# Two graph layers on one Trainium2 core: the first loads reordered, two of the first right sums made by ScalarE and accumulating transfers, and P5 placed between the turnings of the last adjacency chunks

## The chip, the cores and the metric

The kernel runs on one core of a Trainium2 chip. The metric is the time of the whole program on the device in microseconds. Five engines work side by side, each with a queue of its own: TensorE (PE in the profile; PEld is its loading of weights), VectorE (DVE), ScalarE (ACT), GpSimd (POOL) and SyncE (SP). [...]SP, ACT and POOL also issue transfers (DMA), which are carried out apart from the engines.

## The reference

The inputs are x, of shape (16, 1024, 128) in float32, a (1024, 1024) matrix `adj`, and small weights. Both layers are a graph step with a residual and a layer normalization:

```python
def gnn0(x):                       # first layer
    support = einsum('bnf,fo->bno', x, weight)
    return einsum('nm,bmo->bno', adj, support) + bias

def step(h):                       # second layer, 5 times
    m = einsum('nm,bmd->bnd', adj, h)          # both halves of av are this
    av = concatenate([m, m], axis=-1)
    u3 = h @ u3_w.T + u3_b
    z = sigmoid(av @ w3_w.T + w3_b + u3)
    r = sigmoid(av @ w4_w.T + w4_b + u3)
    hv = tanh(av @ w5_w.T + w5_b + (r * h @ u5_w.T + u5_b))
    return (1 - z) * h + z * hv

x = layernorm(x + gnn0(x))
x = layernorm(x + five_steps(x))
```

So each of the 16 batches is multiplied by `adj` six times. The change lies in the very first of these products.

## The kernel before

**Tiling.** The 16 batches go in four groups ("quads") of four. For a quad the product with `adj` is done by a Strassen-like scheme of two levels. At the outer level the matrix is taken as blocks and sums of blocks, `outer[1]` to `outer[7]`: 1 and 2 are the upper blocks, 4 and 7 the lower ones as they come out of the turning, and 3, 5 and 6 are the sums `s4`, `s1`, `s2`. Each outer product is done by an inner level of seven products, P1 to P7, with left sides `left[n][1..7]` and right sides `right[1..7]`. Outer products 1 and 2 are done together by one `chain`; then 3; then 6 and 7; then 5 and 4. PSUM banks `pa`, `pb`, `pc` hold the inner products.

**The right sides.** In the first chain, with `rows` holding x0 to x3 (the four batches of the quad), P1 and P2 read x0 as it is, P3 reads x1 as it is. P5, P6, P7 and P4 read the four right sums, in `inner[0]`, made by `inner_sums` (lines 326 to 331): the first is x1 less x0 (the first block of each, for both halves of the rows), the second is x1's other block less the first sum, the third is x1's other block less x1's first block, the fourth is x0's other block less the second sum. Each is a DVE instruction of 128x512.

**The left sides.** `adj` comes in eight chunks of 512 KB and must be transposed on chip. `turn_adj(c)` does it for one chunk: for each of its two halves, four transposes on PE into a PSUM bank, and one copy from the bank into `blk`, by DVE or by ACT. The banks come from `bank()`, a rotation over three. P1 and P2 need chunks 0 and 1 only. `first_rest` turns chunks 2 and 3, and then `inner_left_12` makes the left sums of outer products 1 and 2 on DVE, four instructions of 128x1024 (lines 188 to 191; the second is the left side of P5, the third that of P6). `turn_rest` turns chunks 4 to 7. `outer_s1` makes `s1` in two halves (line 756; the first reads chunks 4 and 5, the second 6 and 7), line 751 makes `s2`, `outer_s4` makes `s4` in two halves (line 795).

**Sums by transfer.** `added_sums`, `added_left` and `added_t4` make a difference without DVE: ACT writes the negative of one operand, and a transfer issued by POOL adds the other operand to it from memory (`accum_op=ALU.add`). They serve the outer right sums in `tsum` and the left sums in `outer[7]`.

**Order.** [...]`tc.keep_in_program_order(op)` pins `op` behind the instruction that was traced just before it on the same engine; `tc.issue_after` pins a group behind a given one. In the first chain the order of the inner products is (1, 2, 5, 6, 7, 3, 4), and `hooks[12][a]` lists what is called ahead of product `a`. All DVE work named above is pinned, and so are the transposes of chunks 0 to 3; the inner products of the first chain and the transposes of chunks 4 to 7 are not. The copies of line 207 on ACT are not pinned either.

**Loads.** Line 127 issues the first loads: the first six alternate between the queues of SP and ACT, the rest go by SP. In the order of that line, SP issues chunk 0, x0, chunk 2, then chunks 4 to 7, x2, x3; ACT issues chunk 1, x1, chunk 3.

Of the kernel before, what the change touches and what calls it, by code (L numbers as in the profile page):

```python
# [12 lines left out]
ALU = mybir.AluOpType  # L13
# [7 lines left out]
def kernel(  # L21
# [32 lines left out]
    nc = tc.nc  # L54
    B, N, D = x.shape
    P = 128
    C = N // P
# [3 lines left out]
    CH = C // 2  # L61
# [10 lines left out]
    rows = const.tile([P, QUAD, N], F32, name="rows")  # L72
# [5 lines left out]
    inner = [const.tile([P, 4, 2, QT], F32, name=f"inner{i}") for i in range(2)]  # L78
# [16 lines left out]
    def bank(name, i=None):  # L95
        if i is None:
            i = turns[0]
            turns[0] = (i + 1) % 3
        return ps_m.tile([P, HALF], F32, tag=f"g{i}", name=name)
# [15 lines left out]
    def x_rows(b):  # L115
        return x[b].rearrange("(p c) d -> p (c d)", c=C)
# [7 lines left out]
    adj_rows = adj.rearrange("(h p n c) m -> n h p c m", h=2, n=4, c=2)  # L124
    raws = [agg[:, c] if c < CH else hid[:, c - CH] for c in range(C)]

    for i, c in enumerate([0, 1, "x0", "x1", *range(2, C), "x2", "x3"]):
        queue = queues[i % 2 if i < 6 else 0]
        if isinstance(c, str):
            k = int(c[1])  # L130
            queue.dma_start(rows[:, k], x_rows(k))
        else:
            queue.dma_start(raws[c], adj_rows[c // 2, c % 2])
# [10 lines left out]
    s1 = const.tile([P, CH, HALF], F32, name="s1")  # L144
    s2 = const.tile([P, CH, HALF], F32, name="s2")
    s4 = const.tile([P, CH, HALF], F32, name="s4")
    outer = {
        1: blk[0][:, 0], 2: blk[0][:, 1], 3: s4, 4: blk[1][:, 1], 5: s1, 6: s2, 7: blk[1][:, 0],
    }
# [34 lines left out]
    def inner_left_12():  # L184
        a = [[blk[0][:, :, 2 * j : 2 * j + 2, ts(i, QT)] for j in range(2)] for i in range(2)]
        put = tc.keep_in_program_order
        (a11, a12), (a21, a22) = a
        put(nc.vector.tensor_sub(e12[:, :, 3], a11, a21))
        put(nc.vector.tensor_add(e12[:, :, 0], a21, a22))
        put(nc.vector.tensor_sub(e12[:, :, 1], e12[:, :, 0], a11))  # L190
        put(nc.vector.tensor_sub(e12[:, :, 2], a12, e12[:, :, 1]))

    def turn_adj(c):
        cols = raws[c].rearrange("p (q k) -> p k q", k=C)
        i, at = divmod(c, CH)
        for j in range(2):
            pt = bank(f"pt_adj_{c}_{j}")
            pt3 = pt.rearrange("p (k q) -> p k q", k=CH)
            for k in range(CH):
                op = nc.tensor.transpose(pt3[:, k, :], cols[:, j * CH + k, :], ident)  # L200
                if c < CH:
                    tc.keep_in_program_order(op)
            dst = blk[i][:, j, :, ts(at, P)]
            if j == 0 and i == 0:
                tc.keep_in_program_order(nc.vector.tensor_copy(dst, pt3))
            else:
                nc.scalar.copy(dst, pt3)
# [118 lines left out]
    def inner_sums(xs, dst):  # L326

        yield nc.vector.tensor_sub(dst[0], xs(0, 1), xs(0, 0))
        yield nc.vector.tensor_sub(dst[1], xs(1, 1), dst[0])
        yield nc.vector.tensor_sub(dst[2], xs(1, 1), xs(0, 1))  # L330
        yield nc.vector.tensor_sub(dst[3], xs(1, 0), dst[1])

    def blocks_of(src, ns):

        if ns in ((1, 2), (3,)):
            v = src.rearrange("p b (h j x) -> p b h j x", h=2, j=2)
            if ns == (1, 2):
                return lambda j, k: v[:, k, :, j]
            return lambda j, k: v[:, 2 + k, 1:2, j]
        at = {(6, 7): slice(1, 3), (5, 4): slice(0, 4, 3)}[ns]  # L340
        return lambda j, k: tsum[:, at, k, ts(j, QT)]

    def sums_of(src, ns, pinned=False):
        t = inner[0 if ns in ((1, 2), (6, 7)) else 1]
        for op in inner_sums(blocks_of(src, ns), [t[:, i, : len(ns)] for i in range(4)]):
            if pinned:
                tc.keep_in_program_order(op)
        return op

    def first_sums(src):  # L350
        return inner_sums(blocks_of(src, (1, 2)), [inner[0][:, i] for i in range(4)])
# [339 lines left out]
    def call(f, *args):  # L691
        return lambda: f(*args)
# [20 lines left out]
    def added_sums():  # L713


        v = [
            x[2 * i : 2 * i + 2].rearrange("b (p c) d -> p b (c d)", c=C)[:, :, ts(j, HALF)]
            for j in range(2) for i in range(2)
        ]
        (lo, hi), ((lo0, hi0), (lo1, hi1)) = (rows[:, 0:2], rows[:, 2:4]), (v[:2], v[2:])  # L720
        put = tc.keep_in_program_order
        def added(i, negative, rest):
            put(nc.scalar.mul(tsum[:, i], negative, -1.0))
            put(nc.gpsimd.dma_start(tsum[:, i], rest, accum_op=ALU.add))

        added(2, hi[:, :, :HALF], hi1)
        yield
        added_left()
        added(0, lo[:, :, :HALF], hi0)
        yield  # L730
# [12 lines left out]

    rooms = [rows, hid]

    def turn_rest():
        for c in range(CH, C):
            turn_adj(c)
            if c % 2:
                outer_s1(c // 2 - 2)  # L750
        tc.keep_in_program_order(nc.vector.tensor_sub(s2, s1, outer[1]))

    def outer_s1(at):
        cols = ts(at, QT)
        tc.keep_in_program_order(
            nc.vector.tensor_add(s1[:, :, cols], outer[7][:, :, cols], outer[4][:, :, cols])
        )

    def first_rest():
        for c in range(2, CH):  # L760
            turn_adj(c)
        inner_left_12()

    def steps_of_sums(ns):
# [3 lines left out]
    def take(steps, n):  # L768
        for _ in range(n):
            op = tc.keep_in_program_order(next(steps))  # L770
        return op
# [4 lines left out]
    by_transfer = added_sums()  # L776
# [21 lines left out]
    for q in range(NQ):  # L798
        room = rooms[q % 2]
        hooks = {}  # L800
        if q == 0:
            hooks[12] = {
                2: [first_rest],
                5: [turn_rest, call(next, by_transfer)],
                7: [call(outer_s4, 0), call(take, sums3, 1), call(next, by_transfer)],
                3: [call(outer_s4, 1)],
                4: [
                    call(take, steps, 1)
                    for steps in (left3, left3, sums3, sums3, left3, left3, sums3)
                ] + [sum_t2],  # L810
            }
            hooks[3] = {7: [added_t4]}
            hooks[67] = {1: [rest_67]}
            layer0_weights()
            sums_of(rows, (1, 2), True)
        else:
            hooks[12] = projections(q - 1)
            hooks[12][6] += [
                call(sums_of, room, (3,), q == 1),
                call(outer_sums, room, False, True, q == 1),  # L820
            ]
            if q == 1:
                hooks[12][1].append(call(outer_sums, room, "lo", False, True))

        def fetch(q=q):
            drain(99, 0)
            if q == 0:

                for dst, b in [(hid[:, k], QUAD + k) for k in range(QUAD)] + [
                    (ypad[k], k) for k in range(2)  # L830
                ]:
                    tc.keep_in_program_order(nc.gpsimd.dma_start(dst, x_rows(b)))
                load_layer1_weights()
                return
            for k in range(2):
                nc.sync.dma_start(ypad[k], x_rows(q * QUAD + k))
            if q + 1 < NQ:
                load(q + 1, rooms[(q + 1) % 2], x_rows)
            else:
                load(0, rows, saved_rows)  # L840

        def ahead(room):
            with tc.issue_after(last_start[0].ins):
                sums_of(room, (1, 2))
                outer_sums(room, True, False)

        hooks.setdefault(67, {})["end"] = [fetch]
        hooks[54] = {7: [call(ahead, rooms[(q + 1) % 2])]}
        if q == 0:
            steps = first_sums(rooms[1])  # L850
            hooks[54] = {
                7: [call(take, steps, 2)],
                (3, (0,)): [
                    call(take, steps, 2), call(outer_sums, rooms[1], "hi", False, True),
                ],
            }
        if q != 1:
            then = f"12_x{q + 1}" if q + 1 < NQ else "12_0_0"
            hooks[54][4] = [call(head, then, rooms[(q + 1) % 2])]
        if q == 1:  # L860
            hooks[54][5] = [layer1_weights]
            hooks[54][4] = [turn_weights]
        if q == 0:
            aggregate(f"x{q}", room, hooks, False, (1, 2, 5, 6, 7, 3, 4), start_67)
        else:
            aggregate(f"x{q}", room, hooks, False)
# [199 lines left out]
```

## Time and profile before

| what | value |
|---|---|
| time, median of 3 runs | 1766.96 us (1766.76 to 1766.97) |
| the profiled execution: its own time | 1767.13 us |
| its span in the profile | 1764.9 us |
| PE busy | 1753.4 us, 6709 matmuls |
| DVE busy | 1302.2 us, 2286 instructions |
| ACT busy | 800.8 us, 1425 instructions |
| POOL busy | 110.4 us, 153 instructions |
| from start to P1's first matmul | 8.61 us |
| PE's last hole in the first 60 us | 0.60 us, ending at 11.17 us |
| mean granted clock of PE | 0.998 |

The span is what the profiler saw from the first to the last instruction; the program's time has 2.2 us more around it. Rows of a timeline give start, duration, engine, line, operation, output and input, the number of instructions merged into the row, and in brackets the idle time ahead of it and what ended it. Rows of the waits view give who waited for whom, the microseconds in total, the times, and the longest.

### The profile page before, as it was taken

To read this page: it belongs to the slowest core of one execution; us is meant where nothing else is said; L and a number is where in the kernel's file an instruction comes from. 1 tells how busy PE (TensorE), PEld (TensorE's weight loads), DVE (VectorE), ACT (ScalarE), POOL (GpSimd) and SP (SyncE) were. 2 spreads that over 40 slices of the span, in tenths; PEclk is the share of its full clock that TensorE was granted. 3 is DMA by queue.
4 is the path that set the end of the run, shared out by engine and by line. 5 is a ranking of instruction groups with operands and counts; after the bars stand their busy time and mean duration, and the time that the engine had idled before them with its cause. 6 is when DMAs were issued, how large, how long until landed. Compare 5 with 4: busy or idle time off the path is not lost.

```text
span 1764.9 us, 19957 instructions
## 1 busy us (share of the span) xinstructions
PE 1753.4 (99%) x6709; PEld 1264.9 (72%) x6709; DVE 1302.2 (74%) x2286; ACT 800.8 (45%) x1425; POOL 110.4 (6%) x153
## 2 busy tenths in 40 slices
PE   9999999999999999999999999999999999999998
PEld 8888885776858577685867758576675857668584
DVE  7977777676776857777778667777778577777778
ACT  4355554344353433435354452535445353443537
POOL 2312320000000000000000000000000000000004
PEclk9999999999999999999999999999999999999999
DMA  9244354051332505143351424324243240514232
GB/s 266 75 139 144 120 142 109 12 119 34 86 69 67 140 18 136 39 118 75 81 132 60 108 60 96 87 69 119 58 110 101 55 94 26 131 25 107 60 84 95
DMA packets 405604, 161.86 MB, mean 92 GB/s; under 512 B 388352, under 2 KB 389504, under 8 KB 405504
## 3 DMA queue, kind: packets, MB, share of 16 engines
q1 hardware_dynamic: 402960, 153.01, 34.2%
q0 software_dynamic: 1968, 5.77, 1.3%
q10 hardware_dynamic: 576, 1.84, 0.3%
q8 instruction: 53, 0.87, 0.2%
q14 instruction: 47, 0.39, 0.1%
HBM read 94.51 MB, written 65.01 MB: 90 GB/s over the span
## 4 chain that ended last, share of the span: by engine, by line
PE 99%; DMA 1%; DVE 0%; POOL 0%; issue 0%; SPq 0%; POOLq 0%; ACT 0%; DVEq 0%
PE pb L425 25%; PE pc L425 14%; PE pa L425 14%; PE pu L553 8%; PE ph L576 8%; PE ph L577 8%; PE pu L535 8%; PE seeded L568 8%; PE pc_x L425 3%; PE pa_x L425 3%; PE seeded L509 2%; DMA agg<-in_adj_dram 1%; PE pt_adj L200 0%; PE pt L667 0%; PE pt_end L941 0%
## 5 line engine op out<-in xcount | busy, mean ns | idle before, releaser
L425 PE MATMUL pb<-e,inner 128*128 128x256 f32 x864 | 206.2, 379 | 0.0
L592 DVE TENSOR_TENSOR tsum<-tsum,hid 128x512 f32<-128x512 f32 x158 | 108.7, 688 | 106.1 <-ACT tsum L587 106.0
L587 ACT ACTIVATE tsum<-ph,bh 128x512 f32<-128x512 f32 x158 | 108.5, 687 | 164.6 <-PE ph L577 164.5
L425 PEld LDWEIGHTS pb<-e,inner 128*128 128x128 f32 x864 | 167.7, 194 | 19.0 <-ACT first L409 0.3
L553 PE MATMUL pu<-agg,w_t 128*128 128x512 f32 x320 | 163.7, 593 | 0.0
L576 PE MATMUL ph<-agg,w_t 128*128 128x512 f32 x320 | 163.4, 592 | 0.0
L568 PE MATMUL seeded<-agg,w_t 128*128 128x512 f32 x320 | 163.4, 592 | 0.0
L577 PE MATMUL ph<-tsum,u_t 128*128 128x512 f32 x320 | 163.4, 592 | 0.0
L535 PE MATMUL pu<-hid,u_t 128*128 128x512 f32 x320 | 157.0, 592 | 0.0
L556 ACT ACTIVATE tsum<-pu,br 128x512 f32<-128x512 f32 x160 | 110.0, 687 | 85.6 <-PE pu L553 85.6
L425 PE MATMUL pb<-s,inner 128*128 128x256 f32 x576 | 148.0, 379 | 0.0
L425 PE MATMUL pb<-a,inner 128*128 128x256 f32 x576 | 144.0, 379 | 0.0
L563 DVE TENSOR_TENSOR tsum<-tsum,hid 128x512 f32<-128x512 f32 x160 | 110.3, 689 | 38.1 <-ACT tsum L556 38.1
L425 PE MATMUL pc<-e,inner 128*128 128x256 f32 x560 | 133.9, 379 | 0.0
L425 PEld LDWEIGHTS pb<-s,inner 128*128 128x128 f32 x576 | 110.7, 194 | 23.7 <-issue 10.9
L571 ACT ACTIVATE tsum<-seeded,bz 128x512 f32<-128x512 f32 x160 | 110.0, 687 | 29.4 <-PE seeded L568 29.4
L425 PEld LDWEIGHTS pb<-a,inner 128*128 128x128 f32 x576 | 111.8, 194 | 12.7 <-DVE first L411 0.4
L425 PEld LDWEIGHTS pc<-e,inner 128*128 128x128 f32 x560 | 109.2, 195 | 12.8 <-PE pu L535 0.7
L577 PEld LDWEIGHTS ph<-tsum,u_t 128*128 128x128 f32 x320 | 60.8, 190 | 76.5 <-issue 59.1
L576 PEld LDWEIGHTS ph<-agg,w_t 128*128 128x128 f32 x320 | 60.6, 190 | 75.1 <-issue 74.4
L535 PEld LDWEIGHTS pu<-hid,u_t 128*128 128x128 f32 x320 | 60.8, 190 | 73.5 <-issue 72.2
L593 DVE TENSOR_TENSOR tsum<-tsum 128x512 f32<-128x512 f32 x158 | 109.2, 691 | 4.9
(201 smaller groups left out, 2860.9 us busy)
## 6 DMA issues: line engine op xcount, KB each, us to landing
turned<-ypad SPq DMA_DIRECT2D x48, 512.0 KB, 3.8
rows<-turned SPq DMA_DIRECT2D x192, 128.0 KB, 2.9
hvs<-saved SPq DMA_DIRECT2D x24, 512.0 KB, 4.1
rows<-saved SPq DMA_DIRECT2D x20, 512.0 KB, 3.8
hid<-hidden SPq DMA_DIRECT2D x64, 128.0 KB, 3.4
turned<-ypad SPq DMA_DIRECT2D x32, 256.0 KB, 2.9
rows<-turned SPq DMA_DIRECT2D x128, 64.0 KB, 2.1
hidden<-ypad SPq DMA_DIRECT2D x12, 512.0 KB, 4.0
```

Of the source, the lines that this page charges most:

```text
L425: product = nc.tensor.matmul(bank_of[a][:, ts(o, QT)], chunk(a, o, c), left[n][a][:, c, :], start=(a in (1, 5) and o == 0 and c == 0), sto ...
L535: in_order(nc.tensor.matmul(pu, w_t["u3"], hid[:, k, ts(h, HALF)], start=True, stop=True, skip_group_check=True))
L553: in_order(nc.tensor.matmul(pu, w_t["w4"], agg[:, k, cols], start=False, stop=True, skip_group_check=True))
L556: pin(nc.scalar.activation(rh[:, cols], pu, AF.Sigmoid, bias=br))
L563: pin(nc.vector.tensor_mul(rh[:, cols], rh[:, cols], hid[:, k, cols]))
L568: in_order(nc.tensor.matmul(pz, w_t["w3"], agg[:, k, cols], start=False, stop=True, skip_group_check=True))
L571: pin(nc.scalar.activation(z_of[k % 2][:, cols], pz, AF.Sigmoid, bias=bz))
L576: in_order(nc.tensor.matmul(ph, w_t["w5"], agg[:, k, cols], start=True, stop=False))
L577: in_order(nc.tensor.matmul(ph, w_t["u5"], rh_of[k % 2][:, cols], start=False, stop=True))
L587: pin(nc.scalar.activation(hv, ph, AF.Tanh, bias=bh))
L592: pinned(nc.vector.tensor_sub(hv, hv, hid[:, k, cols]))
L593: pinned(nc.vector.tensor_mul(hv, hv, z_of[k % 2][:, cols]))
```

## The change

There are five edits, all of which act on the first quad:

1. The order of the loads: chunk 2 is issued on ACT's queue where x1 was, chunk 3 on SP's where chunk 2 was, and x1 on ACT's where chunk 3 was.
2. The copy of the first half of chunk 3 goes to ACT; those of chunks 0, 1 and 2 stay with DVE.
3. DVE makes only the first two right sums. The third and the fourth are made in `added_right`, called between the turning of chunk 3 and the left sums: ACT writes the negative of one operand, and a transfer issued by POOL adds the other from x in memory.
4. `turn_rest` is cut in two. Chunks 4 and 5 are turned ahead of P5 and the first half of `s1` follows; chunks 6 and 7 are turned ahead of P6, and the second half of `s1` and `s2` follow.
5. The first outer sum by transfer, called ahead of P5 after all of the turning, is now called ahead of P6, again after it.

```diff
-    for i, c in enumerate([0, 1, "x0", "x1", *range(2, C), "x2", "x3"]):
+    for i, c in enumerate([0, 1, "x0", 2, 3, "x1", *range(4, C), "x2", "x3"]):
...
-            if j == 0 and i == 0:
+            if j == 0 and c < 3:
                 tc.keep_in_program_order(nc.vector.tensor_copy(dst, pt3))
             else:
                 nc.scalar.copy(dst, pt3)
...
-    def turn_rest():
-        for c in range(CH, C):
+    def turn_rest(at):
+        for c in range(CH + 2 * at, CH + 2 * at + 2):
             turn_adj(c)
-            if c % 2:
-                outer_s1(c // 2 - 2)
-        tc.keep_in_program_order(nc.vector.tensor_sub(s2, s1, outer[1]))
+        outer_s1(at)
+        if at == 1:
+            tc.keep_in_program_order(nc.vector.tensor_sub(s2, s1, outer[1]))
...
+    def added_right():
+
+        put = tc.keep_in_program_order
+        xs, t = blocks_of(rows, (1, 2)), inner[0]
+        for i, b, negative in ((2, 1, xs(0, 1)), (3, 0, t[:, 1])):
+            half = x[b].rearrange("(p c) d -> p (c d)", c=C)
+            put(nc.scalar.mul(t[:, i], negative, -1.0))
+            put(nc.gpsimd.dma_start(
+                t[:, i], half.rearrange("p (h j x) -> p h j x", h=2, j=2)[:, :, 1],
+                accum_op=ALU.add,
+            ))
+
     def first_rest():
         for c in range(2, CH):
             turn_adj(c)
+        added_right()
         inner_left_12()
...
-                5: [turn_rest, call(next, by_transfer)],
+                5: [call(turn_rest, 0)],
+                6: [call(turn_rest, 1), call(next, by_transfer)],
...
-            sums_of(rows, (1, 2), True)
+            take(first_sums(rows), 2)
```

## The prediction, made before the change was run

> **What bounds the kernel now.** I read the page first: the busy shares and the chain of work that ended last.
>
> ```profile
> span 1764.9 us, 19957 instructions
> PE 1753.4 (99%) x6709; PEld 1264.9 (72%) x6709; DVE 1302.2 (74%) x2286; ACT 800.8 (45%) x1425; POOL 110.4 (6%) x153
> ...
> PE 99%; DMA 1%; DVE 0%; POOL 0%; issue 0%; SPq 0%; POOLq 0%; ACT 0%; DVEq 0%
> ```
>
> TensorE (PE) is the chain for 99% of the span. All edits act in about the first 30 us, so the question is how many microseconds PE's queue shifts there; what follows moves with it. Next, who PE waited for in the first 30 us:
>
> ```profile
> PE pb L212 <- POOL ident masks.py:199: 1.3, 1, 1.3
> PE pa_x L425 <- DMA rows<-in_x_dram: 0.6, 1, 0.6
> PE pt_adj L200 <- DMA agg<-in_adj_dram: 0.6, 1, 0.6
> ```
>
> The third row is the hole between P1 and the turning of chunks 2 and 3. From 11.17 us on PE has no hole. Now the timeline, PE rows:
>
> ```profile
> 8.61 1.96 PE L425 MATMUL pa_x<-a,rows 128*128 128x256 f32 x8 [0.61 <-DMA rows<-in_x_dram]
> 11.17 2.18 PE L200 MATMUL pt_adj<-ident,agg 128*128 128x128 f32 x16 [0.60 <-DMA agg<-in_adj_dram]
> 13.19 1.89 PE L425 MATMUL pa_x<-a,rows 128*128 128x256 f32 x8
> 14.92 4.00 PE L200 MATMUL pt_adj<-ident,hid 128*128 128x128 f32 x32
> 18.76 1.89 PE L425 MATMUL pc_x<-e,inner 128*128 128x256 f32 x8
> 29.51 1.03 PE L425 MATMUL pb<-e,inner 128*128 128x256 f32 x4
> ```
>
> They are P1; chunks 2 and 3; P2; chunks 4 to 7; P5; and, on the last row, P6 of the product that follows (its right side made from x2 and x3; I call it 3.P6). And the timeline of VectorE (DVE):
>
> ```profile
> 9.03 0.69 DVE L328 TENSOR_TENSOR inner<-rows 128x512 f32<-128x512 f32 x1 [0.92 <-DMA rows<-in_x_dram]
> 9.76 0.69 DVE L329 TENSOR_TENSOR inner<-rows,inner 128x512 f32<-128x512 f32 x1
> 10.37 0.68 DVE L330 TENSOR_TENSOR inner<-rows 128x512 f32<-128x512 f32 x1
> 10.97 0.68 DVE L331 TENSOR_TENSOR inner<-rows,inner 128x512 f32<-128x512 f32 x1
> 11.89 0.69 DVE L205 COPY a<-pt_adj 128x512 f32<-128x512 f32 x1 [0.24 <-PE pt_adj L200]
> ...
> 14.01 1.23 DVE L188 TENSOR_TENSOR e<-a 128x1024 f32<-128x1024 f32 x1 [0.53 <-ACT a L207]
> ...
> 18.81 2.35 DVE L756 TENSOR_TENSOR s<-a 128x1024 f32<-128x1024 f32 x2
> ...
> 28.88 0.42 DVE L329 TENSOR_TENSOR inner<-rows,inner 128x256 f32<-128x256 f32 x1
> ```
>
> From 14.01 to past 31 us the waits view names no wait of DVE. Its sum of 28.88 ends at 29.30; 3.P6, which reads it, loads its weights at 29.41. So **DVE has 0.1 us of slack against PE there**: a later DVE chain stops PE. By 40 us the slack is over 2 us, so that is the narrow place.
>
> [...]the L205 copy at 11.89 stands behind four sums. [...]the engines are fully busy at 407 to 419 GB/s from 5.9 to 15 us, so swapping loads speeds up none in total.
>
> **The loads.** Issue time plus time to landing gives: x0 8.4, x1 9.0 (second on ScalarE's queue), chunk 2 11.0 (third on SP's), chunk 3 11.6 (third on ScalarE's), chunk 4 12.5, chunk 7 16.3, x3 18.9. The edit permutes transfers of equal size (512 KB), so I keep the landing times of the places: chunk 2 at 9.0, chunk 3 at 11.0, x1 at 11.6. Each queue issues as many as before; nothing later on SP moves. If the landings of the third pair came in the other order, x1 would be 0.6 us earlier.
>
> **Third chunk early, on PE.** P1 and P2 read x0 only. P1 stays at 8.61 to 10.57. Chunk 2 then fills the 0.60 us hole: gain up to 0.6. Sixteen transposes are 1.92 us (0.12 each), so chunk 2 and half of chunk 3 are through at 12.0.
>
> **The sums behind x1, on DVE.** Two of the four sums stay on DVE and now wait for x1: start 11.65, the second at 12.38 (spacing of 9.03 to 9.76). The DVE copy of chunk 2 is pinned behind them: 12.99 (spacing 0.61) to 13.68. Queued behind that copy on DVE is everything else; waiting for it on PE is the second half of chunk 3. Turning uses three PSUM banks in rotation, two per chunk, so that half takes the bank which this copy empties. Before, it started 0.06 after the copy's end (12.58 to 12.64). Now 13.74, and with its 0.71 us it ends at 14.45 instead of 13.35. ScalarE's copy of it takes 0.58, and the four left sums start at 15.10 instead of 14.01: **1.09 late**. The two sums taken off DVE, 2 x 0.68 us, gain nothing: before they ran while DVE waited for chunk 2. That chunk 3's first copy goes to ScalarE is free: ScalarE is idle in that window but for 0.57 us of P1's copy.
>
> **P5 among the turns.** P2 follows at 14.29 to 16.18, chunks 4 and 5 to 18.0, P5 to 19.73 (8 x 0.216; its left sum is ready 2.39 after 15.10, at 17.49), chunks 6 and 7 to 21.7. ScalarE's last copy lags by 0.70, as before (18.92 to 19.62): 22.4. The second half of s1 on DVE reads that copy. Before it ran at 19.99, so the copy had 0.37 us to spare; P5's 1.73 us ahead of it is far more. DVE gets to it after four left sums and the first half of s1 at 15.10 + 4.80 + 1.18 = 21.08, and waits till 22.45. Delay of everything behind it: 22.45 - 19.99 = **2.46 us**. Queued behind are s2, both halves of s4, the eviction of P7 (L411, which lets P4 start) and the sums of 3.P5 and 3.P6. Less 0.1 of slack at 3.P6, PE is 2.4 us late.
>
> **The accumulating transfers.** ScalarE takes two more ACTIVATEs of 128x512 (0.58 each), behind chunk 3's last copy: 15.1 to 16.3. ScalarE has idle time then (1.14 us ahead of its row at 15.12). POOL issues two transfers of 256 KB, at about 16.0 and 17.2 (its accumulating issues took 0.87 to 1.43); it was idle until 20.89, so no later issue is held, and those come later now anyway, behind chunk 7's copy: tsum's first by 3.0 us with 4.3 us between its landing (26.8) and its reader (31.08) before, the two into the matrix's seventh sum by 1.3 us, less than their reader's shift. The trace has no such transfer beside the load. [...]accumulating transfers of 512 KB landed 5.0 to 9.1 us after issue here[...]. I take 7, so 23.0 and 24.2. P7 needs the first at 24.3, and could start 1.3 us later unnoticed, since its eviction is held by DVE until 27.6; P4 needs the second at 28.3. Cost 0; if the cover is gone, each microsecond costs one. They also take up to 2 x 0.6 us of the engines' time from x2 and x3 (estimate: 512 KB at 417 GB/s), first read at 22.5 now. A gain from them is excluded, since no PE or DVE row waited for the sums.
>
> **Sum.** The hole's 0.6 gained is inside the times above. PE +2.4 us at 29.5 us, nothing given back later since PE has no hole left. The profiled execution took 1767.13 us (span 1764.9 and 2.2 around it), 0.17 over the median of 1766.96. So 1769.5 for it, **1769.4** for the median. A change within 0.2% (3.5 us) is about what a measurement of this kernel can tell from none, so this counts as no change.
>
> **Rivals.** PE's order of unpinned work is made by a planner, which the trace of before cannot show for the new code.
> - P2 goes between the halves of chunk 3, filling the bank wait. P5 then waits for its sum at 17.49, chunk 7's last copy is at 21.9, s1's second half is 1.95 late: PE +1.9, 1768.9. For it: P2 is ready by 11.2. Against it: before, the planner left P2 behind both chunks though PE stood idle.
> - The planner turns chunks 6 and 7 ahead of P5. Then the last copy is at 20.6 and only the 1.09 remains: PE +1.0, 1768.0.
> - The gain: the swap does as its form suggests, x1 early enough (by 9.9 us) not to hold chunk 2's copy, and chunks 6 and 7 ahead of P5. PE -0.6, 1766.4. Against it: 419 GB/s leaves no room for x1 before 11.
> - **Slower beyond the bound:** the transfer for P7 lands late on a crowded queue. It decides from 25.5 us on (9.5 after issue); plain transfers of POOL's queue took up to 11.4 in this trace. At 12 after issue P7 starts at 28.0, its eviction is at 30.0 instead of 27.6: +2.4 more, 1771.8. Beyond 0.2% it counts from 10.6 after issue.
>
> **How the numbers follow.** Chances: my forecast 0.50, P2 moved 0.18, chunks ahead of P5 0.15, gain 0.04, late transfer 0.13. The range goes from 1767.6 (the third case with x1's landing 0.4 earlier) to 1771.2 (half of the late transfer), leaving out the gain and the tails. Slower than 1770.5 takes the late transfer and little else: 0.13. Faster than 1763.4 has no mechanism: 0.01. Same 0.86.
>
> **What would show it.** In the profile after: DVE's first L328 waits for the rows' DMA until about 11.6 and the chunk 2 copy follows at 13.0; PE has a hole or P2 at 12.0 to 13.7; L188 starts at 15.1; L756's second instruction waits on a ScalarE copy until 22.4; P4 waits for L411. The forecast is wrong if L188 starts before 14.0, if DVE has no wait ahead of s1's second half, or if P7 waits for a transfer.

## The result and the profile after

| | before | changed |
|---|---|---|
| median of 22 runs each | 1766.88 us | 1769.37 us |
| lowest to highest | 1766.46 to 1767.37 | 1769.02 to 1771.00 |
| span of the profiled execution | 1764.9 us | 1767.3 us |

The ratio is 1.0015 (95% interval 1.0009 to 1.0021): 2.5 us slower, which is less than 0.2% but clear of the scatter. In the three kernels of this document in which PE stands ahead of the second half of chunk 3, some executions (3 of 22 of the changed kernel, 10 of 18 and 7 of 21 of two below) form a second group about 1.4 us above the first, which moves a median by up to 1.1 us; no execution of it was profiled, so its cause is open.

The page of the changed kernel, head and chain of work:

```profile
span 1767.3 us, 19960 instructions
PE 1754.9 (99%) x6709; PEld 1266.9 (72%) x6709; DVE 1300.4 (74%) x2283; ACT 802.9 (45%) x1428; POOL 113.4 (6%) x155
...
PE 98%; DVE 1%; DMA 1%; issue 0%; ACT 0%; POOL 0%; ACTq 0%; POOLq 0%; DVEq 0%
```

DVE has three instructions fewer (two sums, one copy) and ACT three more, yet DVE has come into the chain with 1% of the span; 9.1 us of that lie in the first 31 us. DVE has less to do and has become more of a bound. Who PE waited for in the first 40 us:

```profile
PE pb L212 <- POOL ident masks.py:199: 1.3, 1, 1.3
PE pt_adj L200 <- DVE a L205: 1.1, 1, 1.1
PE pc_x L425 <- DVE e L175: 0.5, 1, 0.5
PE pa_x L425 <- DVE s L808: 0.3, 1, 0.3
PE pa_x L425 <- DVE a L205: 0.2, 1, 0.2
```

The waits for a DMA are gone from this list. Four waits for DVE have taken their place, 2.1 us in all. The PE rows of the timeline:

```profile
9.34 1.99 PE L425 MATMUL pa_x<-a,rows 128*128 128x256 f32 x8 [0.17 <-DVE a L205]
11.17 1.49 PE L200 MATMUL pt_adj<-ident,agg 128*128 128x128 f32 x12
13.78 0.71 PE L200 MATMUL pt_adj<-ident,agg 128*128 128x128 f32 x4 [1.12 <-DVE a L205]
...
17.93 1.89 PE L425 MATMUL pc_x<-e,inner 128*128 128x256 f32 x8
19.66 2.04 PE L200 MATMUL pt_adj<-ident,hid 128*128 128x128 f32 x16
...
27.31 1.13 PE L425 MATMUL pa_x<-s,rows 128*128 128x256 f32 x4 [0.28 <-DVE s L808]
28.27 1.89 PE L425 MATMUL pb<-a,inner 128*128 128x256 f32 x8
30.67 1.10 PE L425 MATMUL pc_x<-e,inner 128*128 128x256 f32 x4 [0.51 <-DVE e L175]
```

Twelve of the sixteen transposes of chunks 2 and 3 run at once. The last four stand 1.12 us for DVE's copy, which must empty their bank. P5 is at 17.93, chunks 6 and 7 behind it at 19.66. The last three rows are 3.P1, P4 and 3.P5: PE no longer finds its left sums ready. DVE's rows:

```profile
11.71 0.69 DVE L328 TENSOR_TENSOR inner<-rows 128x512 f32<-128x512 f32 x1 [2.42 <-DMA rows<-in_x_dram]
12.43 0.69 DVE L329 TENSOR_TENSOR inner<-rows,inner 128x512 f32<-128x512 f32 x1
13.04 0.68 DVE L205 COPY a<-pt_adj 128x512 f32<-128x512 f32 x1
15.15 1.23 DVE L188 TENSOR_TENSOR e<-a 128x1024 f32<-128x1024 f32 x1 [1.42 <-ACT a L207]
...
19.95 1.22 DVE L756 TENSOR_TENSOR s<-a 128x1024 f32<-128x1024 f32 x1
22.44 1.23 DVE L756 TENSOR_TENSOR s<-a 128x1024 f32<-128x1024 f32 x1 [1.28 <-ACT a L207]
```

Three waits stand in a row: 2.42 us for x1, 1.42 for the copy of chunk 3's second half, 1.28 for chunk 7's last copy. The second half of s1 starts at 22.44. Before it started at 19.94: the merged row of both halves, 18.81 to 21.16, less the 1.22 us of one half. The chain of waits of the first 40 us (start, duration, what) goes through just these:

```profile
2.34 9.27 DMA rows<-in_x_dram
...
11.71 0.70 DVE inner L328
...
12.43 0.69 DVE inner L329
13.12 0.61 DVE a L205
...
13.78 0.71 PE pt_adj L200 x4
...
19.87 0.59 ACT first L408
20.45 1.31 ACT a L207 x3
...
21.78 0.64 ACT a L207
...
22.44 1.24 DVE s L756
```

From x1's landing at 11.6 through two sums and one copy to four transposes; from P5's eviction (L408) and the four copies queued behind it on ACT to the second half of s1.

### The profile page after: what moved, and what is told of

It is laid out like the page before. It is cut to its first block, busy times and chain, and to the rows that moved or that the text cites. A ratio compares the mean times of both kernels' runs of the same rounds, so it can differ in the third digit from the quotient of the medians.

```text
span 1767.3 us, 19960 instructions
## 1 busy us (share of the span) xinstructions
PE 1754.9 (99%) x6709; PEld 1266.9 (72%) x6709; DVE 1300.4 (74%) x2283; ACT 802.9 (45%) x1428; POOL 113.4 (6%) x155
## 4 chain that ended last, share of the span: by engine, by line
PE 98%; DVE 1%; DMA 1%; issue 0%; ACT 0%; POOL 0%; ACTq 0%; POOLq 0%; DVEq 0%
PE pb L425 24%; PE pc L425 14%; PE pa L425 14%; PE pu L553 8%; PE ph L576 8%; PE seeded L568 8%; PE pu L535 8%; PE ph L577 8%; PE pc_x L425 3%; PE pa_x L425 3%; PE seeded L509 2%; DMA rows<-in_x_dram 1%; PE pt L667 0%; PE pt_adj L200 0%; DVE s L751 0%
## 5 line engine op out<-in xcount | busy, mean ns | idle before, releaser
L280 POOL TENSOR_SCALAR rstd<-mv 128x8 f32<-128x8 f32 (+1 forms) x32 | 12.0, 374 | 1611.6 <-DVE mv L269 1550.1
```

## The experiments

To compare them, each has the place of one landmark in the chain of waits: the start of the six matmuls that end the products of the first quad, at 58.60 us before (58.77 when the kernel before was profiled again among these). "PE late" is the difference to 58.60. Each line's median is set against the runs of the kernel before on the same chip in the same batch.

| kernel | PE late at 60 us | median, against before | ratio, 95% interval |
|---|---|---|---|
| changed | 2.09 | +2.5 | 1.0009 to 1.0021 |
| loads only | 2.25 | +3.7 | 1.0012 to 1.0026 |
| right sums only | 0.53 | +0.7 | 0.9997 to 1.0013 |
| P5 among the turnings only | 0.72 | +0.9 | 0.9997 to 1.0013 |
| changed, P5 behind all turnings | 1.15 | +1.4 | 1.0004 to 1.0017 |
| changed, chunk 2's copy on ACT | 0.13 | +0.5 | 0.9995 to 1.0012 |
| the same, P5 behind | 0.03 | +0.4 | 0.9994 to 1.0010 |
| changed, sums behind chunk 2's copy, P5 behind | 0.96 | +0.3 | 0.9993 to 1.0009 |
| loads, copies on ACT, four sums on DVE | 0.03 | +0.2 | 0.9993 to 1.0010 |
| copies on ACT, P5 behind, sums on GpSimd | 1.03 | +1.3 | 0.9999 to 1.0015 |
| copies on ACT, P5 behind, three sums on DVE | -0.72 | -0.5 | 0.9989 to 1.0005 |

The theory: two waits of DVE in series, its copy of chunk 2 behind x1's sums, and the second half of s1 behind chunk 7's copies. The rivals: the accumulating transfers, and a slow start of PE. Eight of the eleven intervals hold 1, so most of these differences in time are not clear of the scatter; what tells the theories apart is where the traces show a wait, and each trace is of one execution. The change's second edit, chunk 3's first copy on ACT, was not run alone.

**The parts alone.** First the loads:

```diff
-    for i, c in enumerate([0, 1, "x0", "x1", *range(2, C), "x2", "x3"]):
+    for i, c in enumerate([0, 1, "x0", 2, 3, "x1", *range(4, C), "x2", "x3"]):
```

> The kernel before with the order of the loads alone changed; all four right sums stay on VectorE. Theory (the copy of chunk 2 on VectorE stands behind the sums that wait for x1): four sums from 11.7 to 14.3, the copy of chunk 2 at 14.3, the left sums (L188) at about 16.4 instead of 14.0, s1's second half 2.4 late, PE +2.3 us: worse than or equal to the whole change. Rival (the accumulating transfers make the loss): no such transfers here, so no loss, and a gain of up to 0.6 from the filled hole. Rival (a slow start of PE makes it): +0.7 at most.

Of its timeline, PE's row of the second half of chunk 3, and then DVE's of the copies and the first left sum:

```profile
14.90 0.71 PE L200 MATMUL pt_adj<-ident,agg 128*128 128x128 f32 x4 [2.67 <-DVE a L205]
```

```profile
14.16 1.28 DVE L205 COPY a<-pt_adj 128x512 f32<-128x512 f32 x2
16.27 1.22 DVE L188 TENSOR_TENSOR e<-a 128x1024 f32<-128x1024 f32 x1 [0.83 <-ACT a L207]
```

The copy at 14.16, the left sums at 16.27, PE 2.25 late: as the theory had it, with no new transfer in the program. The edit that is meant to fill a hole of 0.60 us opens one of 2.67. The profiled execution took 1769.10 us; why the median lies 1.3 us above it is open.

Second, the right sums: `added_right` called in `first_rest`, and

```diff
-            sums_of(rows, (1, 2), True)
+            take(first_sums(rows), 2)
```

> The kernel before with the third and fourth right sums alone made by ScalarE and accumulating transfers; loads and turnings as before. Theory: VectorE loses two sums that it did while it waited for chunk 2, so nothing changes: 0.0 +- 0.2 us, L188 at 14.0. Rival (transfers make the loss): P7 waits for its right sum, +1 us or more.

PE's row of P7 in its timeline:

```profile
23.66 1.97 PE L425 MATMUL pb<-e,inner 128*128 128x256 f32 x8 [0.63 <-DMA inner<-in_x_dram]
```

L188 was at 13.80, but my 0.0 is missed: P7, wanted at 23.0, waited 0.63 us for the right sum by transfer. The rival's mechanism exists, at less than its price of 1 us. (The profiled execution took 1767.95, 0.6 above the median, so in others the wait may be shorter.)

Third, P5 among the turnings: `turn_rest` in two parts and the two hooks as in the change, nothing else.

> The kernel before with P5 alone put between chunks 4, 5 and chunks 6, 7. Theory: P5's 1.73 us stand ahead of chunk 7's last copy, which had 0.37 us to spare; s1's second half goes from 20.0 to about 21.4, PE +0.9 to +1.3 us (the lower if the planner fills P4's wait). Rivals (loads or transfers make the loss): 0.0 us.

DVE's rows of s1 in its timeline:

```profile
18.57 1.22 DVE L756 TENSOR_TENSOR s<-a 128x1024 f32<-128x1024 f32 x1
21.07 1.23 DVE L756 TENSOR_TENSOR s<-a 128x1024 f32<-128x1024 f32 x1 [1.28 <-ACT a L207]
```

DVE waits 1.28 us between the halves of s1, the same as in the changed kernel. PE is 0.72 late, a little under the 0.9 to 1.3 expected: in this execution PE began to turn chunk 2 at 10.94, 0.23 earlier than before. The median is 0.9 up.

**The parts taken back from the change.** P5 behind all turnings again (the two hooks and `turn_rest` of before):

> The changed kernel with P5 put back behind all turnings. Theory: L188 stays at 15.1, s1's second half follows its first half without a wait at 21.1 (1.1 late), PE +1.0 us against before, 1.4 less than the whole change. Rival (transfers or a slow start make the loss): stays at +2.4 us.

DVE's timeline, the first left sum and s1:

```profile
15.16 1.22 DVE L188 TENSOR_TENSOR e<-a 128x1024 f32<-128x1024 f32 x1 [1.43 <-ACT a L207]
...
19.96 2.35 DVE L756 TENSOR_TENSOR s<-a 128x1024 f32<-128x1024 f32 x2
```

The first wait stays, the second is gone (both halves are one row), and PE is 1.15 late instead of 2.09. Next, the changed kernel with

```diff
-            if j == 0 and c < 3:
+            if j == 0 and c < 2:
```

> The changed kernel with the first copy of chunk 2 given to ScalarE too, so that nothing of the turning stands behind x1 on VectorE; P5 still among the turnings. Theory: PE's hole of 1.1 us ahead of chunk 3's second half goes; L188 at 13.4 to 14.1 (ScalarE now makes four copies in a row) instead of 15.15; s1's second half still waits for chunk 7's last copy, at about 21.1 instead of 22.4. PE about +0.9 us against before, 1.2 less than the whole change. Rival (the transfers make the loss): unchanged at +2.4 us.

DVE's timeline, the first left sum and the second half of s1, and PE's row of P7:

```profile
13.27 1.23 DVE L188 TENSOR_TENSOR e<-a 128x1024 f32<-128x1024 f32 x1 [0.16 <-ACT a L207]
...
20.48 1.23 DVE L756 TENSOR_TENSOR s<-a 128x1024 f32<-128x1024 f32 x1 [1.20 <-ACT a L207]
```

```profile
22.94 1.97 PE L425 MATMUL pb<-e,inner 128*128 128x256 f32 x8 [0.60 <-DMA inner<-in_x_dram]
```

One copy moved to ACT brings the left sums from 15.15 to 13.27. The second wait stays, 1.20 us, and P7 now waits 0.60 us for its right sum by transfer. PE is 0.13 late, less than the 0.9 I wrote: I had reckoned with the slower start of PE (P1 at 9.34), and here P1 began at 8.66. The median too is only 0.5 up instead of 2.5: this edit alone undoes most of the loss, though the earlier start of PE has a part in the 0.13. With P5 behind all turnings as well:

> The same, with P5 behind all turnings: both waits of the theory are taken away, the new order of the loads and the transfers stay. Theory: L188 at 13.4 to 14.1, s1 without a wait, so the loss of the change is gone but for the transfers, which now are next: the one for P7 is issued at about 15.0 and lands 8.0 later at 23.0, where P7 wants to start at 22.4 to 23.1. PE -0.3 to +0.6 us. Rival (transfers make the whole loss): +2 us.

PE's row of P7 in its timeline:

```profile
23.17 1.97 PE L425 MATMUL pb<-e,inner 128*128 128x256 f32 x8 [0.73 <-DMA inner<-in_x_dram]
```

Both waits are gone, L188 is at 13.29, and PE is no earlier than before the change: P7 now waits 0.73 us for its transfer, which landed 8.9 to 9.2 us after issue. **The third cover**: with the first two waits removed, the transfer is next.

**Order or load?** The two sums moved behind chunk 2's copy on DVE, which keeps the copy (P5 behind all turnings):

```diff
     def first_rest():
-        for c in range(2, CH):
-            turn_adj(c)
+        turn_adj(2)
+        take(right, 2)
+        turn_adj(3)
         added_right()
```

> The changed kernel with P5 behind all turnings and the two sums left on VectorE moved behind the copy of chunk 2 in its queue; that copy stays on VectorE. If it is the order in VectorE's queue, and not the load on an engine, that holds PE: copy of chunk 2 at about 11.8, sums at 12.4 and 13.1, L188 at about 13.9, no hole of PE ahead of chunk 3's second half, PE -0.3 to +0.6 us as in the kernel with the copy on ScalarE. If it is the load: L188 stays at 15.1, +1.2 us.

DVE's timeline from chunk 2's copy to the first left sum:

```profile
11.54 0.69 DVE L205 COPY a<-pt_adj 128x512 f32<-128x512 f32 x1 [2.58 <-PE pt_adj L200]
12.15 0.68 DVE L328 TENSOR_TENSOR inner<-rows 128x512 f32<-128x512 f32 x1
12.87 0.69 DVE L329 TENSOR_TENSOR inner<-rows,inner 128x512 f32<-128x512 f32 x1
13.66 1.22 DVE L188 TENSOR_TENSOR e<-a 128x1024 f32<-128x1024 f32 x1
```

Same work on DVE in another order: PE's hole is gone and L188 is at 13.66 instead of 15.16. It was the order. (The first sum of x1 began at 12.15 in this execution, behind the copy and with no wait for a transfer, against 11.72 in the one it is compared with: no earlier x1 made the difference.) PE's 0.96 is the transfer once more: in this execution, the slowest of its 13, P7 stood 1.22 us for it.

**What else the new loads could give.** The loads, the copies of chunks 2 and 3 on ACT, four sums on DVE:

> The kernel before with the new order of the loads and the copies of chunks 2 and 3 all on ScalarE; four right sums on VectorE, no new transfers, P5 behind all turnings. Theory: the four sums run from 11.7 to 14.2, the left sums start right behind them at 14.25, 0.25 later than before: PE 0.0 to +0.3 us, and 2 us less than with the loads alone. If a gain of the filled hole were to be had on PE alone: -0.6 us.

L188 was at 14.27 and PE 0.03 late, as written: the sums themselves, behind x1, hold the left sums here, and P4 waits 0.45 us for L411. Then, in the kernel with both waits gone, GpSimd in place of ACT and transfers:

```diff
-        for i, b, negative in ((2, 1, xs(0, 1)), (3, 0, t[:, 1])):
...
+        put(nc.gpsimd.tensor_sub(t[:, 2], xs(1, 1), xs(0, 1)))
+        put(nc.gpsimd.tensor_sub(t[:, 3], xs(1, 0), t[:, 1]))
```

> The new order of the loads, the copies of chunks 2 and 3 on ScalarE, P5 behind all turnings, and the third and fourth right sums made by GpSimd itself (1.4 to 1.6 us each, as its rows of 128x512 at the end of the kernel take) instead of by ScalarE and transfers. Theory (with the two waits gone, the late landing of the transfer for P7 is the third): the sums are there at about 13.2 and 15, P7 does not wait, PE -0.5 to -0.7 us against before, unless GpSimd and VectorE hold each other up. If the transfers were not what held P7: as with the transfers, 0.0 us.

Its timeline, first DVE's rows beside the sums of GpSimd, then those sums:

```profile
11.68 1.80 DVE L328 TENSOR_TENSOR inner<-rows 128x512 f32<-128x512 f32 x1 [3.07 <-DMA rows<-in_x_dram]
...
14.12 1.22 DVE L188 TENSOR_TENSOR e<-a 128x1024 f32<-128x1024 f32 x1
15.26 2.30 DVE L189 TENSOR_TENSOR e<-a 128x1024 f32<-128x1024 f32 x1
```

```profile
11.65 1.28 POOL L763 TENSOR_TENSOR inner<-rows 128x512 f32<-128x512 f32 x1 [10.35 <-DMA rows<-in_x_dram]
14.28 2.19 POOL L764 TENSOR_TENSOR inner<-rows,inner 128x512 f32<-128x512 f32 x1 [1.35 <-DVE inner L329]
```

P7 waited for nothing, so the transfer had held it. But DVE lost 2.2 us: L328 took 1.80 instead of 0.69 and L189 2.30 instead of 1.22, ending 0.55 and 1.09 us after the GpSimd instruction beside it, about as if each had begun only then. L188, which had begun at 14.12, ahead of GpSimd's second sum at 14.28, kept its 1.22 us, and it was that sum which took longer: the one that came second lost. P4 stood 1.82 us for L411. The reservation in what I expected decided it. Last, DVE makes three sums and only the fourth goes by transfer:

```diff
-        for i, b, negative in ((2, 1, xs(0, 1)), (3, 0, t[:, 1])):
+        for i, b, negative in ((3, 0, t[:, 1]),):
...
-            take(first_sums(rows), 2)
+            take(first_sums(rows), 3)
```

> The same, but VectorE makes the first three right sums and only the fourth, for P4, goes by transfer. Theory: the sums run from 11.7 to 13.7, L188 at 13.75 (0.26 earlier than before), P7 waits for no transfer, P4's transfer lands at about 23 to 24 and is wanted at 25.5. PE -0.2 us against before.

DVE's first left sum in its timeline:

```profile
13.52 1.22 DVE L188 TENSOR_TENSOR e<-a 128x1024 f32<-128x1024 f32 x1
```

L188 at 13.52, no wait of PE after P1's, PE 0.72 earlier, median 1766.38 against 1766.92. It is the lowest median of all, but the interval of its ratio holds 1, and of the 0.72 us the span has 0.5 left (1764.4 against 1764.9): that it beats the kernel before is seen in one trace, not shown by the times.

**The start of PE.**

> The kernel before once more, for its profile beside these: its transposes of chunks 0 and 1 began at 5.90 us, while six of the kernels since then have had them at 6.26 to 6.63. If that is chance of an execution, it may come anywhere between here; if the programs cause it, 5.90 again.

PE's timeline, chunks 0 and 1, and P1:

```profile
5.88 2.10 PE L200 MATMUL pt_adj<-ident,agg 128*128 128x128 f32 x16
8.77 1.97 PE L425 MATMUL pa_x<-a,rows 128*128 128x256 f32 x8 [0.79 <-DMA rows<-in_x_dram]
```

5.88 again. But the kernel with three sums on DVE, another program, had 5.89, and the others stand between 6.26 and 6.63; neither answer is settled. The rival is out all the same: in the changed kernel P1 begins 0.7 us late and ends at about 11.2, and twelve transposes later PE still stands 1.12 us for DVE.

## Why the prediction was right

The forecast was 1769.4 with a range of 1767.6 to 1771.2; the median is 1769.37. (The upper end does not follow from its reason: half of the late transfer's 2.4 us gives 1770.6. The median lies inside both.) Step by step:

- **Landings kept by place.** Right: DVE's first sum, for x1, began at 11.71 (11.65 predicted).
- **The copy behind the sums.** Right: 13.04 (12.99), the second half of chunk 3 at 13.78 (13.74), L188 at 15.15 (15.10). The kernel with the sums moved behind the copy shows that it is the order. The copy at 11.89 behind four sums, in the kernel before, was no evidence of it, since that copy waited 0.24 us for PE with the sums done. The changed kernel is: its copy began 1.87 us after the transposes of chunk 2 (11.17), directly behind the second sum. In the kernel that has the sums behind the copy, the copy began 0.63 us after the transposes (10.91 to 11.54).
- **P5 among the turnings.** Right: P5 at 17.93 (18.0), s1's second half at 22.44 (22.45). The delay is 2.50 and not 2.46, because it had been at 19.94 and not at 19.99, and chunk 7's last copy, which ended at 19.62, had 0.32 us to spare, not 0.37. Taking it back alone moved PE from 2.09 to 1.15 late.
- **PE 2.4 late at 30 us.** Missed by 0.3: PE was 2.0 late at 3.P5 and 2.1 at 60 us. I had P4 wait for L411 in the old order. In the changed kernel 3.P1 ran ahead of P4 (27.31 and 28.27), which filled part of that wait, and the waits came at 3.P1 (0.28) and 3.P5 (0.51).
- **Nothing lost later.** Also missed by 0.3: in these two profiles PE is 2.39 late at 1728 us. Two steps of 0.2 us, less one of 0.1 the other way at 135 us, make it; at the two, PE's weight loads waited for an eviction for which they did not wait before:

```profile
235.00 0.73 PEld L425 LDWEIGHTS pb<-s,inner 128*128 128x128 f32 x4 [0.32 <-DVE agg L411]
694.93 0.74 PEld L425 LDWEIGHTS pb<-e,inner 128*128 128x128 f32 x4 [0.31 <-ACT pb L407]
```

Why the evictions were late there is not shown; the other traces have steps of this size too. Nor was it right that PE has no hole left after 11.17: the kernel before has one of 0.30 at 241.14, and the changed one keeps it (0.31). That the median was met to 0.03 us is partly luck, since the two misses cancel; for the profiled execution the sum gave 1769.5, and it took 1769.09.
- **The transfers at no cost.** Right that they cost nothing in the changed kernel, wrong in how long they take: they landed 8.0 and 8.5 us after issue, not 7, which was my estimate from the 5.0 to 9.1 us of the 512 KB transfers. P7's sum was there at 23.96, its weights at 24.16: 0.2 us to spare on PE, not 1.3. In both kernels where the other waits were gone and P7's sum still came by transfer, this was the next bound (P7 waited 0.73 and 1.22 us).
- **P1 at 8.61.** Wrong, at 9.34; hidden by the wait behind it.

The rival orders did not come about: PE's order was P1, chunks 2 and 3, P2, chunks 4 and 5, P5, chunks 6 and 7.

## What to carry to other kernels

Before a load is moved later, look on each engine's queue for what stands behind its first reader: here two sums, early in DVE's queue and themselves not urgent, held a copy whose PSUM bank PE needed. Before work is put between two pieces of another engine's input, compare its length with the spare time of the last piece (here 1.73 us against 0.3). And when waits are removed one by one, name the next cover ahead of time: here it was a transfer that had looked free.

## What was not expected of the hardware

- GpSimd and VectorE were slower side by side. In the kernel with two sums on GpSimd, VectorE's sums took 1.80 and 2.30 us instead of 0.69 and 1.22, and GpSimd's second one 2.19 where its first took 1.28 (the profiler's times for GpSimd are rough). It is one trace, and why they were slower is not shown.
- Accumulating transfers of 256 KB, issued while the loads were still running, took 8.0 us (changed kernel) to 10.1 us (with chunk 2's copy on ACT) from issue to landing; those of 512 KB after the loads took 5.0 us (kernel before) to 10.2 us (changed).
- The same 24 matmuls of line 212, with which PE begins, end early or late: the transposes behind them began between 5.88 and 6.63 us. In the traces of the kernel before and of the changed one the starts of PE's first matmuls are 213 ns apart and then, within one or two of them, about 110; this comes at 5.1 us in the kernel before and at 7.6 us in the changed one. No run here separates chance from the program.
